# A graph attention kernel whose projection is regrouped from 15 products on 512 tokens to 29 products on 1024 tokens

## The chip, the cores and the metric

The kernel runs on one core of one Trainium2 chip. The metric is the device time of one execution in microseconds (us). The engines are TensorE (PE, with its weight loads shown as PEld), VectorE (DVE), ScalarE (ACT), GpSimd (POOL) and SyncE (SP); SP issues nearly all transfers.

## The reference

There are 128 graphs of 64 nodes with 768 features each, so 8192 tokens, and two layers (l = 0, 1). All numbers are float32.

```python
h = relu(layernorm(x))
for l in range(2):
    m_left, m_right = h @ W_left[l].T, h @ W_right[l].T          # per graph [64, 768]
    u_left, u_right = h @ m_left.T / sqrt(768), h @ m_right.T / sqrt(768)
    u = u_left where j >= i (and adj), u_right where j < i (and adj)
    e = exp(u) * adj
    att = e / (sum_j e + 1e-10)
    ctx = att @ (h @ W_lin[l].T + b_lin[l])
    h = relu((ctx - mean) / (std + 1e-3) * ln_a[l] + ln_b[l])
out = x + h
```

## The kernel before, in words

Tokens are cut into NB = 16 blocks of T = 512 (8 graphs). A layer has two passes over all blocks, and PE works through them without a break.

**Pass one** makes `m` = h @ W for the two kinds l (left) and r (right), then the scores and the softmax, and stores the attention in DRAM. A 768 x 768 weight is a 3 x 3 grid of blocks of 256 x 256; a block of tokens is 3 feature chunks by 2 token halves of 256. The plain product of these grids takes 18 block products. The kernel uses a scheme with 15, in which each product multiplies a sum of weight blocks with a sum of token blocks. `ORDER` lists the products: the weight (`w_l`, `w_r`, prepared once for each layer and kept in SBUF), the PSUM bank (X, Y, Z, V), the token operand (a plain part of `ht`, or a sum `ts`), and which outputs of `m` take the bank's contents with which sign. A product is 4 matmuls of 128x128 by 128x256 (L436), which the profile shows as 8 PE instructions. `project(u, k)` runs the 15 products of kind k for block u: first all of l, then all of r. After each product `read` takes the bank out: the first time that an output is touched, ACT writes it (L203); later DVE adds to it (L155). A bank is accumulated into by later products, so those must wait until its reads are done.

The other work is placed by hand in slots: two `run` calls a product execute what `put` has filed under that slot number, in order of the program; where the plan has nothing, one entry of `idle` is taken. Each engine executes its own instructions in that order. SP too executes its transfers in that order, and stands still while the next one's input isn't ready. The slots hold:

- The token sums of the next block on POOL (`put_sums_t`, 11 a block, L155).
- `prepare(u + 1)`: normalisation of the rows (layer 0), four DVE transposes (L380), the store of the transposed block to DRAM (`h<-xb`, L376, four transfers), its reload in another layout (`load_h`, `ht<-h`, L268), the load of the rows of the block after (`load_rows`, L263, eight transfers of 192 KB), the softmax steps of an earlier block with the attention's store (L500, eight small transfers), the adjacency (L404), and in layer 1 `affine` on ACT (L275: six steps that scale, shift and clip `ht`).
- After the first product of a block, the scores of the block before (`scores`, L463) in the bank pair `aux`.

**Pass two** computes h @ W_lin with the same 15 products (L852, weights `w_n`), applies the attention and the normalisation, and leaves rows `z` for the next layer, or the output. During its idle slots in layer 0 the weights of layer 1 are loaded and their sums made on POOL (17 for each kind).

At the start of layer 0 the weights and rows are loaded, four row tiles are turned on PE, and the sums of w_l are made on DVE between the first products.

The functions that the change touches, and what calls them:

Of the kernel before, what the change touches and what calls it, by code (L numbers as in the profile page):

```python
# [17 lines left out]
def kernel(  # L18
# [50 lines left out]
    NBB = T // S  # L69
    adj_t = adj2.rearrange("(n h s) j k i -> n h j s (k i)", h=PAIR, s=Q)  # L70
# [44 lines left out]

    def paced(to, f):

        nc.vector.memset(to, 0.0)
        f()

    def load_w(l, kind):
        v = SRC[kind][l].rearrange("(c p) o -> p c o", p=P)
        t = W[l, kind] = [wpool.tile([P, K2, D], F32, name=f"w_{kind}_{s}") for s in range(len(ORDER))]

        def load(s, i, j):
            nc.sync.dma_start(t[s], v[:, j * K2:(j + 1) * K2, i * D:(i + 1) * D])

        if (l, kind) in ((0, "l"), (0, "r")):
            return [lambda s=s, ij=ij: load(s, *ij) for s, ij in RAW.items()]
        return [lambda s=s, ij=ij: paced(t[s][:, 0, :1], lambda: load(s, *ij)) for s, ij in RAW.items()]  # L130

    def centre(l):

        t = W[l, "n"]
        for j in range(3):
# [9 lines left out]
            idle.extend(none * (6 if j == 0 else 2))  # L145
# [3 lines left out]
            for s in blocks:  # L149
                idle.extend(none * 3)  # L150
                idle.append(lambda s=s, mean=mean: nc.gpsimd.tensor_sub(
# [5 lines left out]
    def sums_w(l, kind, eng):  # L157
        t = W[l, kind]
        return [lambda o=o, s=s, a=a, b=b: added(eng, t[o], s, t[a], t[b]) for o, s, a, b in W_SUMS]
# [14 lines left out]

    def sums_t(key, eng=nc.gpsimd):
        ts = TS[key] = {}

        def one(o, s, m, n):
            t = big.tile([P, K2, TH], F32, name="ts", bufs=13)
# [13 lines left out]
    def read(p, to, i, seen, copied=nc.scalar):  # L193

        what = ORDER[i][3]
        for n in range(0, len(what), 2):
            sign, o = what[n], int(what[n + 1])
# [46 lines left out]
    START = (0, 2, 1, 3)  # L244

    def load_rows(l, u, pool):

        XR[l, u] = []
        if (l, u) == (0, 0):

            rows = x.rearrange("(n k h) s f -> n k (h s) f", k=Q, h=PAIR)
            for g in range(2):
                t = pool.tile([P, 2, H], F32, name="x", bufs=2)
                XR[l, u].extend([t[:, 0, :], t[:, 1, :]])
            for q in START:
                nc.sync.dma_start(XR[l, u][q], rows[0, q])
            return
        for g in range(2):
            t = pool.tile([P, 2, H], F32, name="x", bufs=2)
# [19 lines left out]
    def transpose_rows(l, u, pool):  # L279

        key, xr, todo = (1, l, u), XR[l, u], []
        if l == 0:
# [48 lines left out]
            else:  # L331
# [3 lines left out]
                for q, after in zip(START, START[1:] + (None,)):  # L335
# [3 lines left out]
                    if after is not None:  # L339
                        todo.append(dev[after])  # L340
# [621 lines left out]
```

## The time and the profile before

| | us |
|---|---|
| median of 3 runs | 2751.9 (2751.87 to 2754.58) |
| span of the profiled execution | 2750.9 |
| time of the profiled execution around its span, taken as the difference to the median | about 1.0 |
| PE busy | 2730.4 |
| DVE, ACT, POOL busy | 1345.6, 849.9, 1194.4 |
| pass one of layer 0, first product to last scores | 12.8 to 911 |
| pass two of layer 0 | 911 to 1377 |
| pass one of layer 1 | 1377 to 2271 |

A row of the stages gives, after the stretch, its length, the busy time of each engine with the number of its instructions, the granted PE clock (1.00 is full), the busy share of the core's 16 DMA engines, and the GB/s that they moved. A row of the timeline gives the start and the length in us, the engine, the line, the operation and its tiles (written first, read after the arrow), how many such instructions were merged, and in brackets the idle time ahead of it with what ended it.

### The profile page before, as it was taken

The page shows a single profiled execution, that of the slowest core. Times are in us where ns is not written, and L with a number is a line of the kernel's source. Part 1 is how long each engine was busy: PE and PEld are TensorE (multiplying, and loading weights), DVE is VectorE, ACT ScalarE, POOL GpSimd, SP SyncE. Part 2 cuts the span into 40 slices and gives each one's busy share as a digit, 9 for nine tenths or more (in the row PEclk, how much of TensorE's full clock was granted, in tenths as well). Part 3 has the DMA queues.
Part 4 walks back from the last instruction along what each step waited for, and adds up shares of the span by engine and source line. Part 5 has one row for each costly group of instructions (what it writes and reads, how often), then busy time and mean ns, then how long its engine had stood idle before and what let it go on. Part 6 is the DMA issues. An engine that isn't in the chain of part 4 may idle for free.

```text
span 2750.9 us, 46440 instructions
## 1 busy us (share of the span) xinstructions
PE 2730.4 (99%) x18746; PEld 2343.1 (85%) x18746; DVE 1345.6 (49%) x2266; ACT 849.9 (31%) x1612; POOL 1194.4 (43%) x937
## 2 busy tenths in 40 slices
PE   9999999999999999999999999999999999999998
PEld 8888888888888888888788888888888888888886
DVE  6555445545454333333435444444444335666667
ACT  3222223222221154444621211121122214544443
POOL 3332452223223555555522444223222325887886
PEclk9999999999999999999999999999999999999999
DMA  7434433343332333343555433443344205555555
GB/s 206 118 75 98 123 80 81 91 120 89 76 79 74 102 106 119 119 146 127 150 128 148 100 76 76 109 118 79 76 97 120 61 26 146 161 169 167 169 165 150
DMA packets 234072, 310.82 MB, mean 113 GB/s; under 512 B 54146, under 2 KB 184450, under 8 KB 225666
## 3 DMA queue, kind: packets, MB, share of 16 engines
q1 hardware_dynamic: 233698, 307.45, 41.8%
q8 instruction: 149, 2.44, 0.4%
q14 instruction: 65, 0.53, 0.1%
q10 hardware_dynamic: 160, 0.39, 0.0%
HBM read 202.91 MB, written 104.86 MB: 112 GB/s over the span
## 4 chain that ended last, share of the span: by engine, by line
PE 97%; DVE 1%; ACT 1%; DMA 0%; issue 0%; SPq 0%; DVEq 0%; ACTq 0%
PE X L436 24%; PE V L436 16%; PE X L852 12%; PE Y L436 12%; PE Z L436 8%; PE V L852 8%; PE Y L852 6%; PE aux L463 5%; PE Z L852 4%; PE aux L660 2%; PE aux L683 1%; PE Y L683 0%; ACT xb L316 0%; DVE wm L477 0%; DMA w_l<-in_w_left_dram 0%
## 5 line engine op out<-in xcount | busy, mean ns | idle before, releaser
L155 POOL TENSOR_TENSOR ts<-ht 128x512 f32<-128x512 f32 x441 | 587.0, 1341 | 1223.6 <-DMA ht<-h 565.1
L203 ACT ACTIVATE m<-X 128x512 f32<-128x512 f32 (+1 forms) x256 | 151.6, 592 | 1087.6 <-PE X L436 569.7
L155 POOL TENSOR_TENSOR ts<-ht,ts 128x512 f32<-128x512 f32 x189 | 248.7, 1323 | 135.6 <-PE X L852 60.5
L155 DVE TENSOR_TENSOR m<-m,V 128x512 f32<-128x512 f32 (+1 forms) x256 | 173.3, 677 | 269.1 <-PE V L436 269.0
L155 DVE TENSOR_TENSOR m<-m,X 128x512 f32<-128x512 f32 (+1 forms) x256 | 162.9, 677 | 248.0 <-PE X L436 247.4
L852 PE MATMUL X<-w_n,ts 128*128 128x256 f32 x1024 | 244.3, 380 | 0.8 <-ACT hl L203 0.6
L436 PE MATMUL X<-ts,w_l 128*128 128x256 f32 x1024 | 242.7, 380 | 0.1
L436 PE MATMUL X<-ts,w_r 128*128 128x252 f32 (+1 forms) x1024 | 238.8, 376 | 0.0
L155 DVE TENSOR_TENSOR m<-m,Z 128x512 f32<-128x512 f32 (+1 forms) x128 | 87.5, 683 | 307.7 <-ACT m L203 248.9
L852 PEld LDWEIGHTS X<-w_n,ts 128*128 128x128 f32 x1024 | 191.5, 190 | 33.3 <-issue 3.6
L436 PEld LDWEIGHTS X<-ts,w_l 128*128 128x128 f32 x1024 | 192.0, 190 | 30.1 <-DVE m L155 2.7
L436 PEld LDWEIGHTS X<-ts,w_r 128*128 128x128 f32 x1024 | 192.0, 190 | 26.0
L275 ACT ACTIVATE ht<-ht,b_col,a_col 128x512 f32<-128x512 f32 x192 | 143.5, 804 | 148.8 <-DMA ht<-h 148.8
L852 PE MATMUL Y<-w_n,ts 128*128 128x256 f32 x768 | 182.5, 379 | 0.0
L436 PE MATMUL Y<-ts,w_l 128*128 128x256 f32 x768 | 181.5, 379 | 0.6 <-DVE w_l L155 0.6
L436 PE MATMUL Y<-ts,w_r 128*128 128x252 f32 (+1 forms) x768 | 179.1, 376 | 0.0
L436 PEld LDWEIGHTS Y<-ts,w_l 128*128 128x128 f32 x768 | 145.8, 190 | 20.8 <-DVE w_l L155 1.0
L852 PEld LDWEIGHTS Y<-w_n,ts 128*128 128x128 f32 x768 | 145.8, 190 | 20.4 <-issue 0.6
L436 PEld LDWEIGHTS Y<-ts,w_r 128*128 128x128 f32 x768 | 145.9, 190 | 17.4
L155 DVE TENSOR_TENSOR hl<-hl,V 128x512 f32<-128x512 f32 (+1 forms) x136 | 89.1, 655 | 129.6 <-PE V L852 112.0
L818 POOL TENSOR_TENSOR z<-z,b 128x768 f32<-128x768 f32 x62 | 112.6, 1828 | 76.2 <-DVE z L815 76.2
L203 ACT ACTIVATE hl<-X 128x512 f32<-128x512 f32 (+1 forms) x135 | 77.9, 577 | 219.4 <-PE X L852 216.5
(167 smaller groups left out, 4737.1 us busy)
## 6 DMA issues: line engine op xcount, KB each, us to landing
ht<-h SPq DMA_DIRECT2D x63, 1536.0 KB, 7.1
h<-xb SPq DMA_DIRECT2D x124, 384.0 KB, 6.0
z<-z SPq DMA_DIRECT2D x128, 192.0 KB, 3.1
x<-z SPq DMA_DIRECT2D x128, 192.0 KB, 8.4
x<-in_x_dram SPq DMA_DIRECT2D x120, 192.0 KB, 8.3
xr<-in_x_dram SPq DMA_DIRECT2D x120, 192.0 KB, 3.8
out_dram<-xr SPq DMA_DIRECT2D x120, 192.0 KB, 2.7
adj<-in_adj_dram SPq DMA_DIRECT2D x64, 128.0 KB, 2.7
```

What stands on the lines that cost most here:

```text
L155: (eng.tensor_add if sign == "+" else eng.tensor_sub)(o, a, b)
L203: nc.scalar.activation(to(o), p, AF.Copy, scale=1.0 if sign == "+" else -1.0)
L275: nc.scalar.activation(ht, ht, AF.Relu, bias=cols[1][:, c:c + 1], scale=cols[0][:, c:c + 1])
L436: nc.tensor.matmul(p[:, g], w[ORDER[i][0]][:, c, g * P:(g + 1) * P], b()[t][:, c, :].rearrange(bs, s=S)[:, :, :ns], start=(new and g == c ...
L463: nc.tensor.matmul(p[h * S + e:h * S + e + 32, q, e:e + 95], ht[:, c, b * S + e:b * S + e + 32], mb[:, e:e + 95], start=(c == 0), stop=(c ...
L660: nc.tensor.matmul(cx[k][i, m, :HH], at[j, q, :], hl[j, q, m * HH:(m + 1) * HH], start=True, stop=True)
L683: nc.tensor.matmul(parts[r, k][n][i], at[j, q, :], hl[j, q, cut], start=True, stop=True)
L818: nc.gpsimd.tensor_add(zs[k], zs[k], rows["b"])
L852: nc.tensor.matmul(p[:, n], b[t][:, c, r * P:(r + 1) * P], w[s][:, c, :], start=(i in FIRST and i not in PRELOAD and n == c == 0), stop=(c ...
```

## The change

Pass one now works on superblocks of 1024 tokens (two blocks, U = 0 to 7): 3 x 3 weight blocks by 3 feature chunks x 4 token quarters. A scheme with 29 products takes the place of two times 15. `PRODUCTS` has, for each: the weight operand, the token operand (0 to 11 are plain parts, chunk * 4 + quarter; from 12 on sums), the bank (0, 1, 2), whether the bank starts anew, and the outputs in hexadecimal digits with signs. `W_OPS` and `X_OPS` are the sums of weights (23) and tokens (30), with the product that first needs each. Kinds l and r alternate within a product, so there are four slots to a product.

The weight operands are no longer kept in SBUF for a pass. They are written once to DRAM (`WS`, by `keep_weight`) and streamed for each superblock through a ring of eight tiles that hold both kinds (0.5 MB each): when product i is issued, the tile of product i - 1 is loaded with what product i + 7 needs. In layer 0 the first superblock computes the weight sums on DVE while it runs (`first`) and stores them; for layer 1 POOL computes them in the idle slots of pass two. The SBUF that w_n occupies in pass two (`ROOM`) holds rows and transposed blocks in pass one.

The scores of both blocks of a superblock come together after the next superblock's first product. `prepare` is placed for each block of the next superblock from slot 14 and slot 62, with `load_rows` now ahead of `load_h`; `affine` follows 8 slots after. The centring of w_n moves from POOL to DVE, and its sums alternate between POOL and DVE. Pass two's own products stay.

```diff
+    RINGS = 8
+    W_OPS = ((1, 9, "-", 5, 4), (2, 10, "-", 8, 9), (2, 11, "-", 10, 7), (4, 12, "+", 6, 7), (5, 13, "-", 2, 9),
...
+    X_OPS = ((3, 12, "-", 7, 4), (3, 13, "-", 3, 12), (5, 14, "+", 4, 5), (5, 15, "+", 7, 14), (6, 16, "+", 3, 5),
...
+    PRODUCTS = ((1, 4, 1, True, "+0"), (9, 11, 2, True, "+3+7"), (11, 4, 0, True, "-8"), (7, 13, 0, False, "-b"),
+                (12, 3, 0, True, "-5+6+7+a+b"), (14, 15, 1, False, "-3"), (16, 16, 0, False, "-9"),
+                (10, 17, 2, False, "+b"), (17, 10, 1, True, "-4+6"), (18, 5, 0, False, "-3+9"), (8, 19, 2, False, "+8"),
+                (0, 21, 0, False, "+1-2"), (20, 23, 1, False, "+5"), (21, 24, 1, False, ""), (22, 26, 2, False, "-a"),
+                (23, 28, 0, False, "-9"), (1, 29, 1, False, "+2"), (24, 0, 0, True, "+8-a"), (25, 30, 2, False, "+4-5"),
+                (27, 31, 0, False, "-9"), (28, 33, 2, False, "+a"), (13, 35, 1, True, "+3"), (19, 38, 1, False, "+5"),
+                (3, 39, 1, True, "-7"), (29, 40, 1, False, "+a"), (30, 6, 1, False, "+6"), (31, 9, 0, False, "-0+1"),
+                (2, 36, 2, True, "+0+5"), (4, 41, 1, False, "-5+7"))
+    RING = [wpool.tile([P, 2, K2, D], F32, name=f"wp{i}") for i in range(RINGS)]
+    ROOM = wpool.tile([P, 15 * K2 * D], F32, name="room")
+    WS = [[dram.tile([P, 2, K2, D], F32, name=f"ws{l}_{i}") for i in range(NP)] for l in range(L)]
...
+    def keep_weight(l, ss, kind, i):
+        nc.sync.dma_start(WS[l][i][:, "lr".index(kind)], ss[kind, PRODUCTS[i][0]])
+
+    def stream(l, n):
+        nc.sync.dma_start(RING[n % RINGS], WS[l][n % NP])
...
+    AHEAD_X = 4
+    SLOTS = 4 * NP
+    def put_token_ops(l, U, part):
+        count = {}
+        for op in X_OPS:
+            n = count[op[0]] = count.get(op[0], 0) + 1
+            slot = 4 * (op[0] - AHEAD_X) + n - 1
+            if (slot < 0) == (part == "before"):
+                put(slot + (SLOTS if slot < 0 else 0), lambda op=op: token_op(l, U, op, nc.gpsimd))
...
             def prepare(u):
-                todo = transpose_rows(l, u, sp)
+                todo = transpose_rows(l, u)
                 todo.append(lambda: load_h(1, l, u))
                 if u + 1 < NB:
-                    todo.append(lambda: load_rows(l, u + 1, sp))
-                todo.extend(softmax(u - 2) if u > 1 else [])
-                todo.append(lambda: load_adj(u))
-                todo.extend(none * ((9 if u > 1 else 15) if l else 0))
-                return todo + affine(1, l, u)
-
-            def project(u, k, just):
...
+                    todo.append(lambda: load_rows(l, u + 1))
+                return todo
...
+            def both_scores(U):
+                p = aux(0)
+                for n in range(2):
+                    scores(2 * U + n, p[:, n])
+
+            def project(U, weights, done):
+                bank, seen = {}, (set(), set())
+                for i, (w, t, at, new, what) in enumerate(PRODUCTS):
+                    state = []
+                    for k in range(2):
+                        ns = S - 1 if k and U < NU - 1 else S
+                        if new:
+                            bank[k, at] = (right[:, at - 1] if k and at else
+                                           ps_st.tile([P, 2 * TH], F32, name="V" if k else "XYZ"[at]))
...
+                        wk, tk = weights(i, k), tokens(l, U, t)
+                        for g in range(2):
+                            for c in range(K2):
+                                nc.tensor.matmul(p[:, g], wk[:, c, g * P:(g + 1) * P],
+                                                 tk[:, c, :].rearrange("p (b s) -> p b s", s=S)[:, :, :ns],
+                                                 start=(new and g == c == 0), stop=(c == K2 - 1),
+                                                 skip_group_check=True)
+                            if g == 0:
+                                run(4 * i + 2 * k)
+                        state.append((p, ns))
+                        if i == 0 and k == 1:
+                            if U:
+                                both_scores(U - 1)
...
+                        for kk in range(2) if (i, k) == (0, 1) else (k,) if i else ():
+                            p, ns = state[kk]
+                            read(p, lambda o: M[2 * U + o % 4 // 2][:, o // 4 * K2:(o // 4 + 1) * K2,
+                                                                    o % 2 * 4:o % 2 * 4 + 4, kk, :ns], what, seen[kk])
+                        run(4 * i + 2 * k + 1)
...
+                    done(i)
+
+            def streamed(U):
+                def done(i):
+                    n = U * NP + i - 1 + RINGS
+                    if n < NU * NP:
+                        stream(l, n)
+                return (lambda i, k: RING[(U * NP + i) % RINGS][:, k]), done
+
+            def first():
...
+                put(0, lambda: turn(2), lambda: settle(2))
+                put(1, lambda: turn(3), lambda: settle(3))
+                for i in range(2, NP):
+                    fs = weight_ops(i, "l") + weight_ops(i, "r")
+                    put_all(max(2, 4 * (i - 1) - 3), fs)
+                for n, (s0, s1, s2, s3) in {4: (4, 5, 6, 9), 5: (6, 7, 8, 11), 6: (12, 13, 14, 17),
+                                            7: (14, 15, 16, 19)}.items():
+                    put(s0, lambda n=n: stats(n))
+                    put(s1, lambda n=n: inverse(n))
+                    put(s2, lambda n=n: norm(n))
+                    put(s3, lambda n=n: turn(n), lambda n=n: settle(n))
...
+            for U in range(NU):
+                if U:
+                    weights, done = streamed(U)
+                if l or U:
+                    put_token_ops(l, U, "after")
+                if U + 1 < NU:
+                    def block(n, slot):
+                        u = 2 * U + 2 + n
+                        todo = prepare(u)
+                        load = todo.pop(-2) if u + 1 < NB else todo.pop()
+                        slot = put_all(slot + 1, todo)
+                        slot = max(slot, (86, 99)[n]) if U == 0 and l == 0 else slot
+                        put(slot - 1, load)
+                        if l:
+                            put_all(slot + 8, affine(1, l, u))
+                        if U:
+                            put_all(slot + 1, softmax(u - 4) + [lambda u=u: load_adj(u - 2)])
+
+                    for n, slot in enumerate((32, 60) if U == 0 and l == 0 else (14, 62)):
+                        put(slot, lambda n=n, slot=slot: block(n, slot))
+                    put_token_ops(l, U + 1, "before")
...
-            scores(NB - 1)
-            for f in softmax(NB - 1):
-                f()
+            both_scores(NU - 1)
+            for a, b in zip(softmax(NB - 2), softmax(NB - 1)):
+                a()
+                b()
...
-    pass_one(0, {1: one_aside(0)})
-    pass_two(0, {1: two_aside("l"), 2: two_aside("r")})
-    pass_one(1, {1: one_aside(1)})
+    pass_one(0, {NU - 2: bias_aside(0), NU - 1: one_aside(0)})
+    pass_two(0, {0: two_aside()})
+    pass_one(1, {NU - 2: bias_aside(1), NU - 1: one_aside(1)})
     pass_two(1, {})
```

## The prediction

> **What bounds the kernel now.** I read the busy table, the stages, and then the queues in order of time.
>
> ```profile
> PE 2730.4 (99%) x18746; PEld 2343.1 (85%) x18746; DVE 1345.6 (49%) x2266; ACT 849.9 (31%) x1612; POOL 1194.4 (43%) x937
> ```
>
> ```profile
> core 0: us, PE busy (x) PEld busy (x) DVE busy (x) ACT busy (x) POOL busy (x), PEclk, DMA share, GB/s
> 1500.00:1611.00 111.00, 111.00 (x864) 98.21 (x863) 51.33 (x88) 23.06 (x38) 42.51 (x37) 1.00 0.38 93
> 153.50:163.00 9.50, 9.50 (x46) 8.46 (x46) 6.42 (x14) 3.36 (x5) 0.00 (x0) 1.00 0.82 164
> 219.50:224.00 4.50, 4.50 (x22) 4.01 (x22) 2.39 (x6) 1.18 (x2) 0.00 (x0) 1.00 0.95 343
> 224.00:231.50 7.50, 7.50 (x37) 6.63 (x36) 3.21 (x5) 0.59 (x1) 5.71 (x5) 1.00 1.03 223
> ```
>
> PE sets the time: in two blocks of pass one (1500 to 1611) it is busy for all of it at full clock. Only fewer PE instructions, or idle PE, move the end. The last three rows show what the 38% DMA share hides: transfers come in bursts that fill the 16 engines. They are the store of a transposed block `h<-xb`, its reload `ht<-h`, and the next rows. SP's and ACT's order in one block of layer 1:
>
> ```profile
> 1441.29 5.34 SPq L376 DMA_DIRECT2D h<-xb  x4
> 1452.16 0.35 SPq L268 DMA_DIRECT2D ht<-h  x1
> 1452.56 7.49 SPq L263 DMA_DIRECT2D x<-z  x8
> ```
>
> ```profile
> 1447.43 0.41 ACT L483 ACTIVATE adj<-adj 128x256 f32<-128x256 f32 x1
> 1459.81 1.52 ACT L275 ACTIVATE ht<-ht,b_col,a_col 128x512 f32<-128x512 f32 x2 [11.97 <-DMA ht<-h]
> ```
>
> The reload waits until the store has landed, goes out at 1452.16, and lands at 1459.8, 18.5 us after the store's first issue. ACT stands for 12 us on `affine` and loses nothing: no ACT read of PSUM is due in those products.
>
> **What the Trainium skill says.** "DMA: Bandwidth & Descriptors", *Queues, rings and completion order*: "On each SDMA engine descriptors are consumed in ring order". The trace agrees: the rows issued behind the reload move after it (343 GB/s, then 223). So what SP issues later lands later. "SBUF — State Buffer", *SBUF: two separate sides*: a DVE op with two SBUF inputs and a GpSimd op exclude each other for a whole instruction. The trace agrees: two weight sums on DVE beside POOL took 1.37 and 1.16 us, against 0.684 alone. "ScalarE: Activation LUTs", *What ACT_TABLE_LOAD costs*: about 1283 ns plus a drain. Layer 0 of the trace has 1283 ns loads, and from the softmax add's end (214.53) to the multiply behind exp (216.99) it took 2.5 us.
>
> **The change, part by part.** A product (8 PE instructions) takes 1.727 us for kind l and 1.70 for r, from starts of neighbouring products in order of time. A pair is 3.427 us; it now carries four `run` slots of 0.857 us.
>
> *Removed.* Two blocks needed 30 pairs, a superblock needs 29. 16 superblocks x 3.427 = **54.8 us less**. The two score groups of 4.1 us stay, now together. Pass two's matmuls stay. The last superblock's full-width r products cost 15 more of 0.027 in each layer: 0.8 us.
>
> *Hidden beside PE.* Reads of PSUM go from 36 to 41 for each kind and two blocks: DVE gets 10 more of 0.68 us, 7 us of some 108, DVE stood at 46%. Token sums go from 22 to 30 on POOL, 8 x 1.34 = 11 us, POOL at 38%; they run four products ahead. Streaming is 0.52 MB a product pair; at the 384 GB/s that the weight loads reach at the start this is 1.35 us of DMA in 3.43, which lifts 38% to about 78%. The 46 weight sums on POOL in pass two (34 before) and 58 writes of 0.26 MB lie beside a PE that is full, at a DMA share near 0.4. If a cover fails, PE waits; where it can is costed next.
>
> *First superblock.* Product 0 needs only quarter 0, two row tiles, and can start near 10.5 us instead of 12.8: x0, x1 and one weight block come first, and DVE's statistics and PE's turns take what they take now. But six turns (0.87 us each) now stand among the products: +5.2. Weight sums for both kinds fall on DVE early (46 x 0.69 in all), beside POOL's sums and thus sometimes twice as long; I allow 2 us over the 3 us that the old start lost. Sum **+5** (0 to 15).
>
> *Reload in layer 1, first block of a pair.* T (the store's issue) is where the fourth transpose ends. The transposes sit in slots 15, 17, 19, 21, each behind DVE's reads of products 4 and 5; adding 0.65 a read and 0.9 a transpose from product 3's start gives T = 11.4 us = slot 25. On DMA then, from 1.4 us after T: the store 8.3, one streamed weight 1.35, the rows 7.2 (now ahead of the reload in SP's order), the reload 4.0, and 0.8 to land: **23.0 us after T** instead of 18.5, slot 52. `affine` is in slots 33 on, so ACT stops there. Behind its first two steps in ACT's order stands the first write of output 4 from product 8, kind r. Product 12 adds into the same bank and cannot start before this read is done: slot 52.4 + (1.6 + 0.6 + 0.2) us = slot 55, against slot 50. PE waits 4.3 us; I take 4 (0 to 7). Seven times: **+28**.
>
> *Late weight in layer 0, first block.* Transposes in 33 to 39 compete with products 8 and 9, two DVE reads each kind: T = slot 44.6. The weights of product 17 are issued after store, rows and reload (slot 43, store in 41): 1.4 + 8.3 + 7.0 + 4.0 + 1.35 + 0.8 = 22.85 us after T; needed in slot 68, 20.0 us after T. Late by 2.8; I take 2.5 (0 to 5), six times: **+15**. The same sum for the second blocks gives 0.6 (layer 0) and 1.1 us (layer 1), less than its own error: half of 6 x 0.6 + 7 x 1.1, **+6** (0 to 25).
>
> *Softmax in layer 0, second block.* It falls in slots 92 to 99, where products 21 to 25 all use the same bank of each kind, so one DVE read must end within 1.7 us of a product. Two steps of 1.12 us stand before one such read; the multiply waits 2.4 us for exp and its table before another, with 0.85 + 0.9 us of DVE work behind it. By adding up, PE loses 0.5 + 1.8 = 2.3; I take 1.5 (0 to 3), six times: **+9**.
>
> *Ends.* Two softmax chains now stand together at each pass's end. ACT's read of pass two's product 0 waits behind both exps: 1.12 + 0.43 + 0.41 us later, where 0.3 us was lost before: 1.7 x 2. The weight set for pass two, with its centring on DVE, is now put wholly into the last superblock: 2 us a layer. **+7** (2 to 15).
>
> Sum: -54.8 + 0.8 + 5 + 28 + 15 + 6 + 9 + 7 = +16. The profiled span is 2750.9, the median of the runs 2751.9, so 1.0 lies around it: 2750.9 + 16 + 1 = **2768 us**.
>
> **Rivals.** (1) *The lateness is absorbed, faster.* If the reload lands by 18.6 us after T and the stream by 20, the two largest stalls are gone. For it: at 78% the DMA engines have room over a superblock, and the old `affine` was met by a reload just in time. Against: the old trace shows share 1.03 for the rows, which now come first. Left are 54.8 - 0.8 - 5 - 7 = 42, less 9 + 6 at most: 2710 to 2725, say 2716. It decides as soon as the stalls of the bursts sum to less than 37 us. (2) *The stalls balance the saving.* Reload and stream each late by half of my figure: 58 becomes 29 to 37 us with some of the start: within 5 us of 2752. (3) *The first superblock is the bound.* Freed tiles are reused for sums as soon as their write to DRAM is read out; a write stands behind rows and stores on SP for 5 to 10 us. If DVE waits so for four of 46 sums, 20 to 30 us more: 2790 to 2800. Against: few sums remain after product 20. (4) *29 products are not 29.* PE's instructions should be 18746 - 16 x 2 x 8 + 4 x 6 = 18514; if they are not, no gain exists at all. I give it no chance of its own.
>
> **How the numbers follow.** A measurement of this kernel tells about 0.2%, 5.5 us, from no change. My forecast (bursts bind) has 0.47 and rival 3 has 0.10: slower 0.57. Rival 2: 0.11. Rival 1: 0.32. The range leaves a tenth out on each side: 2712, where nearly no stall appears, to 2798, where the late loads take their upper bounds in part (28 and 15 become 49 and 30 at most) or rival 3 comes in.
>
> **What would show it.** PE idle before the product 12 matmuls of kind r in layer 1, released by ACT's `m` read, with ACT idle 15 to 20 us on DMA `ht<-h` before its affine step; PE idle before product 17 in layer 0, released by DMA of the streamed tile; the reload landing about 23 us after the store's first issue; superblocks of 108 us where no stall falls. If the PE is busy at 99% or more in pass one of both layers, the forecast is wrong and rival 1 holds. If idle PE is mostly before 130 us, rival 3 holds.

## The result, and the profile after

The changed kernel takes **2991.23 us** (median of 4 runs, 2983.55 to 2992.70) against 2751.9 before: ratio **1.0864, interval 1.0848 to 1.0879**, slower by 239 us. The forecast was 2768 us, with a range up to 2798. The side was right, the size was not. The profiled execution has a span of 2989.7 us and took 2991.47.

The busy table after:

```profile
PE 2741.9 (92%) x18514; PEld 2336.0 (78%) x18514; DVE 1483.1 (50%) x2469; ACT 847.2 (28%) x1635; POOL 1333.4 (45%) x1036
```

PE has exactly the 18514 instructions that the prediction counted, so the 29 products are 29. But PE is idle for 2989.7 - 2741.9 = 247.8 us, against 20.5 before. And it is busy for 2741.9 us where 2730.4 - 54.8 + 0.8 = 2676.4 would do, 65.5 us more for the same instructions. By the trace's clock record PE was busy for 103 us at half clock, which makes about 52 of the 65.5; before, it was never busy at half clock. The other 14 us were not taken apart. The balance closes: -54.0 (saved) + 227.3 (more idle) + 65.5 (slower work) = +238.8, the difference of the spans.

PE's waits in the whole span (engine, its line, what it waited for; us in total, times, longest):

```profile
PE aux L559 <- DVE m L234: 137.1, 29, 18.7
PE aux L500 <- issue: 45.2, 29, 3.9
PE X L1043 <- ACT hl L316: 17.1, 3, 11.4
PE X L1043 <- POOL ts L234: 7.5, 1, 7.5
```

Before, the scores' wait on "issue" (PE waits for nothing that the profile names) was a single small row:

```profile
PE aux L463 <- issue: 3.4, 7, 1.4
```

L559 is `project`, L500 the scores (L463 before), L1043 pass two's product; further down, L316 is ACT's read of PSUM, L234 a sum (on DVE also the later reads), L393 `affine`, and on SP L444 the store, L381 rows, L386 the reload and L210 the stream. To see where they lie, the two kernels are set side by side at points that both have, the starts of the score groups (from the traces):

| stretch | before, us | after, us | difference |
|---|---|---|---|
| start to the scores of the first superblock | 126.7 | 172.1 | +45.4 |
| layer 0, seven further superblocks | 780.4 | 812.6 | +32.2 |
| end of pass one, pass two, first superblock of layer 1 | 579.1 | 624.5 | +45.4 |
| layer 1, seven further superblocks | 780.7 | 880.0 | +99.3 |
| the rest | 484.0 | 500.5 | +16.5 |

The first point differs a little: the kernel before has one score group (4.1 us) more behind it and one product of kind r (1.7 us) less, so the first stretch lost some 2 us more than the row says and the last some 2 us less.

**Layer 1, the row of two blocks** (columns as in the stage table before):

```profile
1500.00:1625.00 125.00, 110.41 (x849) 96.95 (x848) 45.90 (x67) 22.26 (x37) 39.08 (x32) 0.95 0.68 218
```

PE is no longer busy throughout, and the DMA share is 0.68 where 0.38 stood (0.78 was forecast). The order on SP in the block that starts there:

```profile
1514.17 4.64 SPq L444 DMA_DIRECT2D h<-room  x4
1518.90 1.85 SPq L210 DMA_DIRECT2D wp<-ws  x1
1520.80 6.73 SPq L381 DMA_DIRECT2D room<-z  x8
1527.64 0.36 SPq L386 DMA_DIRECT2D ht<-h  x1
```

Store, one streamed weight, rows, and only then the reload, as forecast. ACT, DVE and PE over the same time, each from its own timeline:

```profile
1536.51 1.52 ACT L393 ACTIVATE ht<-ht,b_col,a_col 128x512 f32<-128x512 f32 x2 [16.36 <-DMA ht<-h]
1537.93 0.57 ACT L316 ACTIVATE m<-aux 128x504 f32<-128x504 f32 x1
```

```profile
1538.54 0.68 DVE L234 TENSOR_TENSOR m<-m,aux 128x504 f32<-128x504 f32 x1 [17.66 <-ACT m L316]
```

```profile
1524.48 1.89 PE L559 MATMUL Z<-ts,wp 128*128 128x256 f32 x8
1539.27 3.73 PE L559 MATMUL aux<-ts,wp 128*128 128x252 f32 x8 [12.89 <-DVE m L234]
1542.79 2.46 PE L559 MATMUL X<-ts,wp 128*128 128x256 f32 x8
```

ACT stands on the reload; behind two steps of `affine` it reads product 8 of kind r; DVE's read of the same bank comes after that; PE stops for 12.89 us ahead of product 10, kind r. Seven such stalls of 12.2 to 13.7 us make 91.1 us. The matmuls after one are slow too: 3.73 and 2.46 us for what takes 1.86 and 1.89 otherwise, about 2.4 us lost. The granted clock (the third column from the end) in the stall, just after it, and later:

```profile
1530.00:1536.00 6.00, 0.00 (x0) 0.00 (x0) 0.00 (x0) 0.00 (x0) 0.00 (x0) 0.52 0.99 349
1541.00:1543.00 2.00, 2.00 (x6) 1.58 (x6) 1.18 (x2) 0.32 (x1) 0.00 (x0) 0.50 0.14 55
1545.00:1547.00 2.00, 2.00 (x11) 1.77 (x10) 0.00 (x0) 1.10 (x3) 0.57 (x1) 1.00 0.42 164
```

The Trainium skill, "TensorE: Matmul & The Clock Gate", *What's actually happening*, says that a gate halves the array's clock when it has been idle and gives it back after some microseconds of work. This trace agrees: 0.52 in the stall, 0.50 from 1.7 to 3.7 us after it, 1.00 from 5.7 us on. The same page gives an idle stretch of about 3.4 us as the condition; here shorter pauses were enough, as the last section shows. The prediction priced every stall at its length alone.

**Layer 0: the scores.** A pair of score groups was 8.2 us of matmuls. Now PE's timeline in one superblock of layer 0 reads:

```profile
748.58 4.44 PE L500 MATMUL aux<-m,ht 128*32 128x95 f32 x205
755.46 4.44 PE L500 MATMUL aux<-m,ht 128*32 128x95 f32 x128 [2.44 <-issue]
761.66 1.33 PE L500 MATMUL aux<-m,ht 128*32 128x95 f32 x51 [1.76 <-issue]
```

That is 14.4 us: 4.2 in two pauses that no semaphore explains, and 1.9 more since the 128 matmuls between them run at 35 ns each, where the first 205 took 22, and the last 51 at 26. Around such a pause in the superblock before (same columns as above):

```profile
636.00:639.00 3.00, 0.76 (x34) 0.54 (x23) 0.00 (x0) 0.00 (x0) 2.84 (x4) 1.00 1.01 392
639.00:642.00 3.00, 2.77 (x76) 2.77 (x79) 0.00 (x0) 1.08 (x2) 2.92 (x3) 0.57 1.02 419
```

The DMA engines are full (1.01, 1.02). The two pauses lie 128 matmuls with 128 weight loads apart: 256 instructions. The Trainium skill, "Runtime: NRT & Kernel Launch", *Instruction fetch mechanics*, says that an engine's instructions come in blocks of 256 over a DMA queue of its own, and that the crossing is "mostly hidden". The spacing agrees, and the profile of this run lists such a queue (transfers, MB, share of the 16 engines):

```profile
q8 instruction: 148, 2.42, 0.3%
```

These 148 transfers have 16 KB each, and the trace has the time of each. All 29 pauses of the scores end 1.2 to 1.5 us after one of them is through (for the pause that ends at 755.46, it ran from 753.19 to 754.25). So PE waits for instructions. In nine of layer 0's 13 pauses the transfer starts only when PE already stands, up to 1.5 us later; in 15 of layer 1's 16 it starts 1.1 to 2.3 us ahead of the pause, and those pauses are 0.3 to 1.2 us long. The DMA share, taken from 3 us ahead of the pause to its end, is below 0.5 in 13 of these 15. Hidden the fetch is in neither case; full engines make it later.

**The first superblock and pass two.** PE's largest gap of all, and what DVE did just before:

```profile
149.64 1.29 DVE L234 TENSOR_TENSOR wp<-room,wp 128x512 f32<-128x512 f32 x2 [19.48 <-DMA ws<-wp]
```

```profile
151.58 3.50 PE L559 MATMUL aux<-ts,wp 128*128 128x252 f32 x8 [18.71 <-DVE m L234]
```

A weight sum waits 19.48 us until the tile that it overwrites has been written to DRAM, PSUM reads stand behind it in DVE's order, and PE stops: rival 3. In pass two of layer 0 two stalls stand out:

```profile
1032.89 3.78 PE L1043 MATMUL X<-room,ts 128*128 128x256 f32 x8 [7.55 <-POOL ts L234]
1437.77 3.78 PE L1043 MATMUL X<-room,ht 128*128 128x256 f32 x8 [11.37 <-ACT hl L316]
```

### The profile page after: what moved, and what is told of

It reads as the page before. It is cut to its first block, busy times and chain, and to the rows that moved or that the text cites. A ratio compares the mean times of both kernels' runs of the same rounds, so it can differ in the third digit from the quotient of the medians.

```text
span 2989.7 us, 47185 instructions
## 1 busy us (share of the span) xinstructions
PE 2741.9 (92%) x18514; PEld 2336.0 (78%) x18514; DVE 1483.1 (50%) x2469; ACT 847.2 (28%) x1635; POOL 1333.4 (45%) x1036
## 4 chain that ended last, share of the span: by engine, by line
PE 75%; DMA 8%; DVE 5%; issue 3%; ACT 2%; SPq 2%; POOL 1%; DVEq 0%; ACTq 0%; POOLq 0%
PE aux L559 14%; PE X L1043 11%; PE Y L559 8%; PE X L559 8%; PE V L559 7%; PE V L1043 7%; PE Z L559 5%; PE Y L1043 5%; PE aux L500 4%; PE Z L1043 4%; DMA wp<-ws 3%; DMA ht<-h 2%; PE aux L851 2%; DVE m L234 2%; DMA room<-z 1%
## 5 line engine op out<-in xcount | busy, mean ns | idle before, releaser
L234 POOL TENSOR_TENSOR ts<-ht 128x512 f32<-128x512 f32 x352 | 476.5, 1359 | 294.1 <-PE aux L559 157.6
L234 POOL TENSOR_TENSOR ts<-ht,ht 128x512 f32<-128x512 f32 x128 | 164.6, 1296 | 936.2 <-PE aux L559 351.5
L559 PE MATMUL aux<-ts,wp 128*128 128x252 f32 (+1 forms) x1872 | 456.7, 389 | 123.0 <-DVE m L234 122.3
L559 PEld LDWEIGHTS aux<-ts,wp 128*128 128x128 f32 x1872 | 364.0, 196 | 181.2 <-DVE m L234 134.6
L234 POOL TENSOR_TENSOR ts<-ht,ts 128x512 f32<-128x512 f32 x192 | 254.4, 1329 | 166.7 <-PE aux L559 94.9
L234 DVE TENSOR_TENSOR m<-m,aux 128x504 f32<-128x504 f32 (+1 forms) x304 | 200.6, 673 | 247.0 <-ACT m L316 126.8
L234 DVE TENSOR_TENSOR m<-m,X 128x512 f32<-128x512 f32 x160 | 105.2, 682 | 400.5 <-ACT m L316 357.5
L1043 PE MATMUL X<-room,ts 128*128 128x256 f32 x1024 | 250.4, 387 | 17.6 <-POOL ts L234 7.5
L559 PE MATMUL Y<-ts,wp 128*128 128x256 f32 x1112 | 263.3, 380 | 1.0 <-DVE m L234 1.0
L1043 PEld LDWEIGHTS X<-room,ts 128*128 128x128 f32 x1024 | 195.0, 193 | 52.0 <-POOL ts L234 12.4
L559 PEld LDWEIGHTS Y<-ts,wp 128*128 128x128 f32 x1112 | 211.9, 191 | 29.6 <-issue 1.4
L393 ACT ACTIVATE ht<-ht,b_col,a_col 128x512 f32<-128x512 f32 x192 | 141.9, 803 | 248.5 <-DMA ht<-h 248.5
L500 PE MATMUL aux<-m,ht 128*32 128x95 f32 x6144 | 147.2, 256 | 45.2 <-issue 45.2
L1043 PE MATMUL Y<-room,ts 128*128 128x256 f32 x768 | 183.2, 380 | 0.0
L500 PEld LDWEIGHTS aux<-m,ht 128*32 128x32 f32 x6144 | 137.3, 116 | 56.6 <-issue 56.5
L234 DVE TENSOR_TENSOR m<-m,Y 128x512 f32<-128x512 f32 x176 | 118.2, 679 | 123.6 <-PE Y L559 108.1
L559 PE MATMUL Z<-ts,wp 128*128 128x256 f32 x736 | 174.3, 380 | 1.6 <-DMA wp<-ws 1.6
L1043 PEld LDWEIGHTS Y<-room,ts 128*128 128x128 f32 x768 | 146.7, 191 | 20.8 <-issue 0.6
L559 PEld LDWEIGHTS Z<-ts,wp 128*128 128x128 f32 x736 | 139.4, 190 | 21.5 <-DMA wp<-ws 3.1
L234 POOL TENSOR_TENSOR ts<-ts,ht 128x512 f32<-128x512 f32 x96 | 122.3, 1274 | 67.6 <-PE V L559 52.5
L234 DVE TENSOR_TENSOR hl<-hl,V 128x512 f32<-128x512 f32 (+1 forms) x136 | 88.9, 654 | 125.7 <-PE V L1043 113.6
L559 PE MATMUL X<-ts,wp 128*128 128x256 f32 x616 | 148.6, 385 | 0.0
```

The source lines that it names most:

```text
L234: (eng.tensor_add if sign == "+" else eng.tensor_sub)(o, a, b)
L393: nc.scalar.activation(ht, ht, AF.Relu, bias=cols[1][:, c:c + 1], scale=cols[0][:, c:c + 1])
L500: nc.tensor.matmul(p[h * S + e:h * S + e + 32, q, e:e + 95], ht[:, c, b * S + e:b * S + e + 32], mb[:, e:e + 95], start=(c == 0), stop=(c ...
L559: nc.tensor.matmul(p[:, g], wk[:, c, g * P:(g + 1) * P], tk[:, c, :].rearrange("p (b s) -> p b s", s=S)[:, :, :ns], start=(new and g == c ...
L1043: nc.tensor.matmul(p[:, n], b[t][:, c, r * P:(r + 1) * P], w[s][:, c, :], start=(i in FIRST and i not in PRELOAD and n == c == 0), stop=(c ...
```

## The experiments

Each is the changed kernel (2991.23 us) with the edit shown. "Gain" is against it, and is known to about 5 us. In brackets stands the 95% interval of the ratio to the kernel before.

**1. `affine` later in layer 1.**

```diff
-                            put_all(slot + 8, affine(1, l, u))
+                            put_all(slot + (29, 26)[n], affine(1, l, u))
```

> The changed kernel with one edit: in layer 1 the six affine steps of a block follow 29 slots (first block of a superblock) or 26 slots (second) after the reload's slot, instead of 8. Theory A (ACT stands on the reload, product 8's first write of kind r stands behind it on ACT, DVE's read of the same bank stands behind that, and PE stops at product 10, kind r): the seven stalls of 12.2 to 13.7 us before that product go, with the slow clock after each (8 PE instructions took 3.7 us instead of 1.9), so 7 x about 15.5 = 108 us less, about 2883 us, PE idle near 135 us. Rival B (the DMA burst itself is late, so that the next streamed weight or a token sum stops PE instead): the stalls move to product 13 or later and at least 5 us of each stay, 2915 us or more.

Measured: 2909.91 us (1.0559 to 1.0590), gain 81 where 108 was expected. All seven stalls are gone, so theory A holds; but rival B is in part true as well. A late weight stops PE ahead of product 13 in each of the seven superblocks, by 2.7 to 3.9 us, here the first wait of PE from 1600 to 2280:

```profile
PE Y L559 <- DMA wp<-ws: 21.1, 8, 3.9
```

In the changed kernel that wait is 0.6 us in the same time: the longer stall covered it.

**2. The same stalls from the other end.** `affine` stays; in layer 1 DVE makes the first write of product 8, so ACT has no read of it.

```diff
-    o % 2 * 4:o % 2 * 4 + 4, kk, :ns], what, seen[kk])
+    o % 2 * 4:o % 2 * 4 + 4, kk, :ns], what, seen[kk],
+    nc.vector if i == 8 and l else nc.scalar)
```

> The changed kernel with one edit: in layer 1 the first write of output 4 from product 8 is made by DVE and not by ACT; affine stays where it is, so ACT stands on the reload as long as before (16 us). Theory A: nothing that DVE does then depends on ACT before product 11, whose two first writes on ACT come late; the bank of product 11 is next used by product 15, in slot 60, when the reload (landing about slot 52) is long in. The stalls go as in the run with the late affine: about 2885 us, with ACT's wait on the reload unchanged in the groups. Rival B (late transfers): no change, 2990. Rival C (the two PSUM tiles of kind r share one buffer, so that any late read of one half stops products in the other): stalls stay but start at product 12 or later, 2920 to 2960.

Measured: 2911.48 us (1.0569 to 1.0600), gain 80, short of the expected 106 by the same late weight (26.5 us in eight waits from 1500 to 2290). ACT's waits on the reload are no shorter (265 us in all, 249 in the changed kernel), and PE no longer feels them. The link is shown: reload, ACT, its read of product 8, PE.

**3. Reload ahead of the rows on SP.**

```diff
-                        put(slot - 1, load)
+                        if U or l:
+                            plan[slot - 1].insert(len(plan[slot - 1]) - (u + 1 < NB), load)
+                        else:
+                            put(slot - 1, load)
```

> The changed kernel with one edit: SP issues the reload of the transposed block before the rows of the block after, as the kernel before did, except in layer 0's first superblock. Theory A: in layer 1 the reload lands 18 to 19 us after the store's first issue and not 22.3, so each stall before product 10 shrinks by about 4 us: 7 x 4 = 28 us less, about 2963. What could take it back: SP now stands about 5 us on the store's landing with streamed weights behind it, which adds a late weight of 1 to 3 us in places: 2960 to 2980. Rival (the order in the burst does not matter): 2991 within 5.

Measured: 3016.9 us (1.0945 to 1.0979), a loss of 26 where a gain of 28 was expected. After the first block of layer 1 the affine stalls shrink to between 7.8 and 10.1 us. But SP now stands on the store's landing with the rows and the stream behind it, and PE stops elsewhere: 2.6 to 4.8 us ahead of product 17 in six superblocks of layer 0 (four times released by a streamed weight, twice by DVE's row statistics), 2.3 to 3.7 us on a weight ahead of product 25 in five of layer 1. Putting the reload first again doesn't win the time back; it moves the wait.

**4. Scores split**: block one's after product 0, block two's after product 1.

```diff
-                        if i == 0 and k == 1:
+                        if i < 2 and k == 1:
...
-                                both_scores(U - 1)
+                                if i == 0:
+                                    pair = aux(0)
+                                scores(2 * U - 2 + i, pair[:, i])
...
```

> The changed kernel with one edit: the scores of the two blocks are no longer made in one go after product 0 but one after product 0 and the other after product 1 (the reads of product 1 then follow its second kind). Theory D (PE runs out of instructions: 1536 short ones in a row take about 8.2 us unhindered, and the fetch of more shares the DMA engines with a burst): half of the row at a time leaves time to refill, each score group takes 4.1 to 4.6 us in layer 0 as in the kernel before, the gaps named issue go, and 7 x (14.2 - 8.6) = 39 us in layer 0 and about 7 x 1.8 = 13 in layer 1 are saved: 2940 us. Rival (the score matmuls wait for data or for a bank): the length of the two groups together stays 14 us, 2990.

Measured: 2968.9 us (1.0776 to 1.0814), gain 22, under half of what was expected. The median time of a superblock in layer 0 falls from 115.7 us to 113.2. PE's wait on issue falls from 45.2 us to

```profile
PE aux L500 <- issue: 20.2, 11, 4.1
```

Shorter runs of short matmuls outrun PE's instruction supply less often, but still do: these 11 pauses too end 1.3 to 1.5 us after an instruction transfer. (The 1536 short instructions of the expectation are 384 matmuls and 384 weight loads in the trace.)

**5. Weight writes of layer 0 on ACT's queue.**

```diff
-        nc.sync.dma_start(WS[l][i][:, "lr".index(kind)], ss[kind, PRODUCTS[i][0]])
+        (nc.sync if l else nc.scalar).dma_start(WS[l][i][:, "lr".index(kind)], ss[kind, PRODUCTS[i][0]])
```

> The changed kernel with one edit: in layer 0 the 58 writes of weight operands to DRAM are issued by ACT's queue and not by SP's. Theory E (in the first superblock DVE's weight sums wait for a freed tile, whose write stands on SP behind stores, rows and reloads that wait for their own inputs): DVE's wait of 19.5 us on these writes and PE's gap of 18.7 us before 152 us shrink to a few, the first superblock ends 15 to 25 us earlier, 2965 to 2975 us. Rival (the DMA engines are the limit there, whoever issues): within 5 us of 2990.

Measured: 2965.48 us (1.0757 to 1.0793), gain 26. The first superblock's scores start at 154.7 us, not 172.1. The 18.7 us stall becomes one of 7.2 on a streamed weight, and the stall of 7.5 at 63 us becomes 3.7. So in the changed kernel the writes were late because they stood on SP behind the store, the rows and the reload. What is left of the start (154.7 against 126.7) was not taken apart.

**6. No streaming after each layer's first superblock.** The ring is filled up to the end of the first superblock only; later superblocks multiply with whatever weight operands the ring then holds.

```diff
-                    if n < NU * NP:
+                    if n < NP:
```

> The changed kernel with the weights streamed only up to each layer's first superblock after their making; later superblocks use what lies in the ring, so their products use wrong weights. This takes 0.5 MB for each product pair out of the DMA queue and nothing else. Theory D (the score gaps come from the fetch of PE's instructions behind a full DMA queue): with the store, the rows and the reload alone, which end before slot 116, the two score groups take 8.2 to 9.5 us in layer 0 from the third superblock on instead of 14.2, layer 0's superblocks 109 to 110 us instead of 115.7. Theory A: the reload in layer 1 lands only 1.4 us earlier, as one streamed weight stood before it, so six of the seven stalls before product 10 stay at 10 to 12 us. About 2991 - 40 - 6 x 3 = 2930 us. Rival (streaming itself is what made the reload late): the stalls of layer 1 fall below 6 us, 2870 or less.

Measured: 2935.1 us (1.0650 to 1.0682), gain 56. Layer 0 runs at 110.7 us a superblock with scores of 9.2 to 11.4 us. But the seven stalls of layer 1 stay: 13.8 us the first, 10.4 to 11.0 the others, 1.5 to 2.8 less than with the stream:

```profile
PE aux L559 <- DVE m L234: 65.6, 11, 11.0
```

(PE's waits, 1520 to 2300.) The stream's transfers make up most of what the scores of layer 0 cost more; they are not what makes the reload late. Some pauses stay without them, 20.6 us of issue in all.

**7. The second block's burst earlier in layer 0.**

```diff
-                    for n, slot in enumerate((32, 60) if U == 0 and l == 0 else (14, 62)):
+                    for n, slot in enumerate((32, 60) if U == 0 and l == 0 else (14, 62) if l else (14, 44)):
```

> The changed kernel with one edit: in layer 0 from the second superblock on, the work on the second block of the next superblock begins in slot 44 and not 62, so that its store, rows and reload (slots 71, 72) are through by about slot 104, a dozen slots before the scores. Theory D: the score groups fall from 14.2 us to 8.5 to 10 us, superblocks of layer 0 from 115.7 to about 110, 6 x 5.5 = 33 us less, about 2958. Rows for that block are asked for in slot 42 and needed from slot 45 on, so DVE and ACT may stand on them for up to 15 us: if PE feels this, the gain is smaller or gone. Rival (the score gaps have another cause): the gaps named issue stay at 2 to 4 us a superblock.

Measured: 3044.65 us (1.1041 to 1.1074), a loss of 53. The scores take 8.5 to 10.9 us in four of the six superblocks concerned, as expected, and 12.4 and 14.7 in the last two. But the statistics of the rows now come before the rows. DVE, and then PE, at the first of six such places:

```profile
229.54 1.02 DVE L351 BATCH_NORM_STATS2 st<-room 128x6 f32<-128x384 f32 x2 [10.61 <-DMA room<-in_x_dram]
```

```profile
234.40 3.75 PE L559 MATMUL Y<-ts,wp 128*128 128x256 f32 x8 [10.48 <-issue]
```

The waits call PE's stop "issue"; DVE's read of PSUM at 233.61, done just before PE goes on, stood behind those statistics.

**8 and 9. Edits together**: 1, 4, 5 and 7, then without 7.

> The changed kernel with four edits together: late affine, split scores, weight writes on ACT's queue, early burst in layer 0. If the causes are separate and their costs add: 81 + 22 + 25 us as measured each for itself, and 10 to 30 of the early burst beyond the split: 2830 to 2855 us. If they share one cause (PE's slow clock after any long stall, or DMA backlog that moves on to the next place): 2870 or more. In no theory below the kernel before, since the ends of the passes (45 us) and the first superblock's other stalls stay.

Measured: 2948.3 us (1.0684 to 1.0736), far from the 2830 to 2855 of separate causes.

> The changed kernel with three edits: late affine, split scores, weight writes on ACT's queue in layer 0 (the run with four edits without the early burst). If their gains add: 2991 - 81 - 22 - 26 = 2862 us. If the losses share a cause, such as one DMA backlog that moves on, 2885 or more.

Measured: 2880.77 us (1.0449 to 1.0490), gain 110 of the 129 that the three give alone, between the two forecasts. The late weight ahead of product 13 is still there, 2.4 to 4.0 us. Edit 7 costs 68 here, so it is what run 8 failed by.

**10. Run 9, and in layer 1 the rows 16 slots after the store**, out of the reload's way.

```diff
+                        rows = todo.pop() if l and u + 1 < NB else None
                         slot = put_all(slot + 1, todo)
+                        if rows:
+                            put(slot + 15, rows)
```

> The three edits, and in layer 1 the rows of the block after are asked for 16 slots later than the store, so that store and reload stand alone in the DMA queue. Theory F (what is left in layer 1, 3.1 us before product 13 in each superblock and the slow clock behind it, is the streamed weight that stands in the queue behind store, rows and reload, as forecast for layer 0): the weight then lands about 7 us earlier, the gap goes, superblocks of layer 1 go from 115.5 to 109 to 111 us, 7 x 5 = 35 us less than with the three edits. Against it: SP stands some 5 us on the store's landing with weights behind it, which in the run with the reload first cost 2 to 3.6 us at another product; then no gain or a loss of up to 10.

Measured: 2864.82 us (1.0391 to 1.0429), 16 better than run 9, where 35 was expected. The wait ahead of product 13 falls to at most 2.4 us.

**11. Pass two's weight sums one block later**, without the pauses between them.

```diff
-                    idle.extend(none * min(len(ops), 1))
...
-    pass_two(0, {0: two_aside()})
+    pass_two(0, {1: two_aside()})
```

> The changed kernel with one edit: in layer 0's pass two the weights of layer 1 are loaded and summed from the second block on (with the empty slots between the sums left out, to fit). Theory G (at the pass's start POOL stands on the raw weights, whose loads stand on SP behind 16 attention stores, and the token sums of the second block stand behind that on POOL): PE's gap of 7.5 us near 1033 and the slow clock after it go, 8 to 11 us less, about 2981. Rival (the token sums wait for the reload of the block itself): within 4 us of 2991.

Measured: 2973.11 us (1.0792 to 1.0825), gain 18 where 8 to 11 was expected; what the rest comes from was not looked into. The 7.5 us stall is gone: POOL had stood for 40 us on the loads of weights, which SP issued only after 16 attention stores, with token sums queued behind:

```profile
1003.62 10.25 SPq L537 DMA_DIRECT2D att<-wm  x16
```

```profile
1025.67 1.26 POOL L234 TENSOR_TENSOR wp<-wp 128x512 f32<-128x512 f32 x1 [40.24 <-DMA wp<-in_w_left_dram]
```

(Both from the timeline of the changed kernel.)

**12. Edits 1, 4, 5, 10 and 11 together**, the best version found.

> The three edits, the rows later in layer 1, and the weights of layer 1 from pass two's second block on. If all add: the run with the rows later less 10 us, about 2815 to 2850. It stays above the kernel before (2752), because about 35 us of the first superblock, 15 to 25 at the end of layer 0's pass two and 4 to 5 us in each superblock of layer 0 are untouched.

Measured: 2853.93 us (1.0351 to 1.0385): 137 better than the changed kernel, just outside the expected 2815 to 2850, and still 102 worse than before. PE's waits:

```profile
PE aux L559 <- DVE m L234: 26.5, 21, 4.4
PE aux L500 <- issue: 20.6, 12, 4.0
PE Y L559 <- DMA wp<-ws: 20.5, 12, 7.4
PE X L1047 <- ACT hl L316: 15.8, 3, 9.9
```

(L1047 is here pass two's product.)

After the first 155 us no stall above 4.4 us remains in pass one; idle PE is 126.5 us, mostly in small parts, and PE is busy for 2727.3 us, 51 above the 2676.4 (33 of it by half clock). No run gave a version that beats the kernel before.

**13 and 14. Why product 10, and not 12.** Two causes could stop PE early in layer 1: DVE's reads behind ACT's (run 13 takes this away), or the two halves of `right`, the PSUM tile that holds banks 1 and 2 of kind r, being waited for as one (run 14 changes what shares it).

```diff
-                (17, 10, 1, True, "-4+6")
+                (17, 10, 1, True, "+6-4")
```

> Changed kernel with one edit: product 8's outputs are listed as +6-4 instead of -4+6, so DVE's read of its bank comes ahead of ACT's in program order; nothing else moves. Theory A (the order of the two reads of one bank sets the stop; DVE no longer stands): PE stops at product 12 of kind r instead of product 10, two products or 6.9 us later, so the seven layer 1 stalls go from 13 to about 6 us, released by ACT's read, and the time falls by about 48 us, to 2943. Theory B (the two halves of `right` are waited for as one tile): PE still stops at product 10 of kind r, now released by ACT's `m` read, the stalls stay at 12 to 13 us, and the time stays within 10 us of 2991.

Measured: 2981.73 us (1.0821 to 1.0853), gain 9.5, as theory B has it. DVE's reads of products 8 and 9 and of product 10, kind l, no longer wait for ACT, and PE stops where it did:

```profile
1531.48 3.73 PE L559 MATMUL aux<-ts,wp 128*128 128x252 f32 x8 [12.99 <-ACT m L316]
```

```diff
-                            bank[k, at] = (right[:, at - 1] if k and at else
+                            bank[k, at] = (right[:, (1, 0)[at]] if k and at < 2 else
```

> Changed kernel with one edit: for kind r, bank 0 takes the place of bank 2 as the other half of `right`, and bank 2 takes the single bank V. The read order of product 8 stays. Theory A (only DVE's order holds PE): the stop moves from product 10 of kind r to product 11 of kind l, so the stalls shrink from 13 to about 11 us, 12 us less in all, about 2979. Theory B (halves are waited for as one tile): product 9 of kind r now writes the other half of product 8's tile, so PE stops there, two turns earlier: stalls of 16 to 17 us, 24 us more from the seven, and a few tenths of a us more wherever banks 0 and 1 follow each other: 3015 or more.

Measured: 3031.46 us (1.1001 to 1.1038), a loss of 40. The stop moves one product forward, to product 9 of kind r (`aux<-ht,wp`):

```profile
1552.73 3.73 PE L559 MATMUL aux<-ht,wp 128*128 128x252 f32 x8 [12.09 <-DVE m L234]
```

Its length stays at 11.3 to 14.9 us, less than the 16 to 17 expected, and new stalls of 2.6 to 2.9 us come in where banks 0 and 1 follow each other. Both runs say the same of the place: a write to one half of `right` waits for a pending read of the other half. Whether the program's semaphores or the chip ask for this isn't told apart.

## Why the prediction was right or wrong

**Right.** The saving (18514 instructions); the order on SP; ACT's stop of 16.36 us (15 to 20 forecast); the landing of the reload, 1536.5 - 1514.2 = 22.3 us after the store's first issue (23.0 forecast); its reach to PE through the read of product 8. "What SP issues later lands later" is more than the ring order that it is drawn from: the Trainium skill, "DMA: Bandwidth & Descriptors", *Queues, rings and completion order*, adds that completion isn't first in, first out for an issuing engine. In this case it held: by the traces' landings none of SP's 1084 transfers before and 1781 after landed ahead of one issued earlier. The late weight of product 17 in layer 0 is there in one superblock only, 0.9 us (2.5 in six taken); 0.8 us ahead of it in another was released by DVE. The softmax of layer 0's second blocks costs 0.8 us in four of them (1.5 in six taken).

**The step that failed: "Product 12 adds into the same bank and cannot start before this read is done: slot 52.4 + (1.6 + 0.6 + 0.2) us = slot 55, against slot 50."** Counted from the store's issue T, the end of the stall was right: slot 55 is 25.7 us after T at slot 25, and PE went on at T + 25.1. Its beginning was wrong. Product 10 of kind r is at slot 42, eight slots ahead of product 12, 6.9 us; it writes the other half of `right`. And T itself came late: it fell 14.2 slots, 12.2 us, ahead of slot 42, so at slot 27.8 instead of 25, which is 2.4 us. So 4.3 + 6.9 + 2.4 - 0.6 = 13.0 us a time, against a mean of 13.0 measured. The bound of 7 us for the term came from the landing's error alone; where PE stops was not bounded at all. Runs 13 and 14 show the place; runs 1 and 2 show the whole: about 80 us net, +28 forecast.

**A term that was missing: the clock.** About 52 us of PE time by the clock record, as much as the saving. A stall of 13 us costs its length and then some 2.4 us. How the 52 us divide among the places was not worked out.

**First superblock, +5 with a bound of 15.** From the saving of 3.4 to +45.4 is 49 us, or 51 with the difference of the two points. Rival 3 had the mechanism (a freed tile waits for its write, the write waits on SP) and 20 to 30 us for it, but was given 0.10. Its counter-argument, "few sums remain after product 20", looked at the sums; one is enough if DVE's PSUM reads stand behind it.

**Scores, no change.** "The two score groups of 4.1 us stay, now together" failed: 12 to 15 us in most of layer 0 and about 10 in layer 1 (once 14.8), instead of 8.2. "If a cover fails, PE waits" asked where data are late; it didn't ask for the instructions. Layer 0's seven superblocks gave +32 instead of -24, and the scores are 36 of these 56 us; the rest was not taken apart. In layer 1 the account comes close: -24 saved, 108 for the seven stalls with their slow clock and 16 for the scores make 100, and 99.3 was measured.

**Ends, +7.** ACT's read behind the exps was right in kind and larger in size (2.88 and 2.87 us, of which 0.3 was there before, against 1.7). The loads behind 16 stores (7.5) and the 11.4 us stall before layer 1 (ACT's `hl` read behind its `z` step, which waits 14.0 us for a transfer that stands on SP behind 12.2 us of row loads) were not in the list; the second was read off the trace and not tested. The 2 us taken in each layer for pass two's weights, with their centring on DVE, came out as 2.65 and 4.41 us, but not by the centring: the DVE work just ahead of the late PSUM read is the sums of w_n (L234, `room<-room`), half of which the change gave to DVE.

Rival 1 (2716) died on all of these. It needed the transfers to be hidden on average, and at a share of 0.68 there is room for them; the stalls come from what stands behind the few that are late. The side of the forecast was right; the +16 came from terms that were mostly far too small, and the largest of them, +28, from the wrong product.

## What to carry to other kernels

A wait on one engine is priced at PE by walking its in-order queue to the first PSUM read behind it, and from that to the first matmul that writes anything in the same tile, not only the same bank. A kernel with PE at 99% has no slack for a stall, and one of more than about 2.3 us here could cost the clock as well as its length, so a saving of 2% in matmuls is lost to fewer than five stalls of 13 us. Added DMA traffic has to be held against everything else that its queue and the engines carry, the instructions included.

## What the runs showed that was not expected

- After a 12.9 us stall the clock stayed at 0.50 for the first 3.7 us of work at least and was 1.00 after 5.7; in the scores it fell to 0.57 (mean of 3 us) after a pause of only 2.5 us.
- The clock record of the changed kernel moves in steps of 3.41 us. Laid on this grid, each of the 27 steps from full to half clock follows a step in which PE was busy for at most 1.39 us, and no step with 1.43 us or more was followed by half clock. The clock came back after steps with 2.88 us or more, and not after 2.46 or less. So not the length of one pause decides, but the work in a step: pauses of 2.3 us were enough at times. The line lay between 1.4 and 1.5 us in eight of the experiments' traces too, but for one step of 1.65 us in run 12.
- Bursts of 128x95 matmuls with a weight load each stood for 0.2 to 3.9 us for the transfer of their next 256 instructions, longest while data filled the DMA engines: 45.2 us in all, 20.6 us when the weights were not streamed.
- DVE's read of product 8 waited for ACT's read of the same bank although the outputs differ; with the order turned round (run 13) ACT's wait no longer reached DVE. Whether the program or the chip asks for that order isn't told apart here either.
